# An attention, feed-forward and expert kernel: hidden features of the early expert tiles turned by transfers, routing tables made in parts

## Chip, cores and metric

The kernel runs on one core of a Trainium2 chip. The metric is device time in microseconds, the median of the runs of a kernel. All arithmetic is in float32.

## What is computed

The reference, cut to what matters:

```python
# x: 2048 x 256, ctx: 1601 x 256
y = layernorm(x)                                 
y = layernorm(y + causal_attention(y, y, y), g1, beta1)
y = layernorm(y + attention(y, ctx, ctx), g2, beta2)
y = layernorm(y + relu(y @ w1 + b1) @ w2 + b2, g3, beta3)
x = x + y
h = layernorm(x)
probs = softmax(h @ wg.T)                         # 8 experts
topk_w, topk_idx = top_k(probs, 2)
topk_w = topk_w / sum(topk_w)
out = x + sum over the 2 chosen e of topk_w[e] * ((silu(h @ w1[e].T) * (h @ w3[e].T)) @ w2[e].T)   # w1, w3: 512 x 256 each
```

The change is in the last line, the experts, and in the tables that say which rows go to which expert.

## The kernel before

**Blocks.** The 2048 rows are four blocks of 512. Self-attention, cross-attention and the feed-forward part run block by block. The last block's feed-forward runs in two halves of 256 rows (`ffn`, line 592); its second half is the last thing on TensorE before the expert stage, and its normalisations on VectorE and GpSimd run on into that stage.

**Routing.** `route(b)` (line 699) makes a block's logits on TensorE and its two best experts on VectorE. For the last block it first turns the normalised rows with eight TensorE transposes (line 256) that ScalarE copies out of PSUM (line 257), then makes 16 small matmuls (line 711). `place(b)` (line 768) counts with two matmuls (lines 772 and 773) at which slot of its expert each row goes, and returns eight scatters ("puts", line 805) on GpSimd's queue that write the rows into the table `slots` in DRAM. From the counts, `tables_0`, `tables_a` and `tables_b` (lines 919, 927 and 933) make small tables on VectorE: for every tile of 128 slots its expert and its first row. `tables_b` is for the tiles that can be filled only when the last block is placed.

**The expert stage.** `run` (line 1192) goes over 37 tiles: a0 to a16 (numbers 0 to 16; full tiles that are known before the last block), p0 to p7 (17 to 24; partly filled ones) and b0 to b11 (25 to 36). For tile n it does, in the order of the program: the first hidden product h1 (`hidden`, four matmuls of 128 x 512, line 1084) and its SiLU on ScalarE into g; the fetch of tile n+3 on SyncE's queue (`fetch`, four transfers of rows and one of weights and row numbers); the second hidden product h3; on VectorE the multiplication of g by h3; then `between(n)`, the turn of tile n+2's rows (`turn_in`, a VectorE transpose within blocks of 32 x 32, line 1066), and the loading of expert numbers for tile n+1.

**Turning g.** The output product (`product`, line 1122, eight matmuls into y) needs g with its 512 features on the partitions. The kernel before has two ways:

- `turn_out` (line 1114): four TensorE transposes into a PSUM bank gtp, and a copy by ScalarE. TensorE does them between h1(n) and h3(n) for tile n-1, and product n-1 follows h3(n).
- `send_across` and `turn_sent` (lines 1096 and 1106): four transfers of 64 KB from ScalarE's queue carry quarters of g across the partitions into gb, and VectorE turns gb in blocks of 32 x 32 into gT. Here g is written with its features in another order, so SiLU and multiplication work on rearranged views. The product of tile n-2 comes between h1(n) and h3(n): one tile later than in the first way.

The set `sent` (line 1023) says which tiles go the second way: 8 to 35. Tile 36, the last, always goes the first way.

**Who orders what.** TensorE's order is the program's throughout. On VectorE, ScalarE and SyncE the compiler chooses the order by its own estimate, until `run` reaches tile SENT = 8 (line 1198); from there on these three run in the program's order. GpSimd's order is the compiler's throughout, with `tc.issue_after` setting single instructions behind others.

**The last block among the tiles.** `between(n)` (line 1249) calls `route` of the last block at n = LATE = 2 and `place` and `tables_b` at n = PUT = 4, so that TensorE meets the routing work after those tiles. Of the eight puts, two are issued after each of tiles 5 to 8, behind the latest indirect add of a product into the output (line 1135, GpSimd's queue). Tables of the last block are first used by the fetch of tile 17, in the turn of tile 14.

**SyncE.** `keep` (line 681) writes the sums xf of the last block to the output; the adds of all expert tiles wait for it.

Of the kernel before, what the change touches and what calls it, by code (L numbers as in the profile page):

```python
# [15 lines left out]
P = 128  # L16
# [3 lines left out]
def xattn_ffn_moe(  # L20
# [46 lines left out]
    NBT = NF_MAX - NA  # L67
    AHEAD = 3
    MORE = 2
    LATE = 2  # L70

# [764 lines left out]
    def filled(n, b):  # L838


        cnt = table(f"cnt{n}", [E])
        nc.vector.tensor_sub(cnt, carry[b], region)
        ge = table(f"ge{n}", [E, NT], tag="ge")
        nc.vector.tensor_tensor(
            ge,
            cnt.unsqueeze(2).to_broadcast([P, E, NT]),
            full.unsqueeze(1).to_broadcast([P, E, NT]),
            ALU.is_ge,
        )
        f = table(f"f{n}", [E])  # L850
        nc.vector.reduce_sum(f, ge, axis=AX.X)
        return f
# [21 lines left out]
    def first_rows(n, ex, k, many):  # L874
        r = table(f"row{n}", [many])
        nc.vector.scalar_tensor_tensor(r, ex, float(REG), k, ALU.mult, ALU.add)
        return r
# [11 lines left out]
    def behind_done(n, f, done, many):  # L889


        left = table(f"left{n}", [E])
        nc.vector.tensor_sub(left, f, done)
        run = running(n, left)
        ex, k = spread(n, run, left, many)
        same = table(f"same{n}", [many, E])
        nc.vector.tensor_tensor(
            same,
            ex.unsqueeze(2).to_broadcast([P, many, E]),
            expert.unsqueeze(1).to_broadcast([P, many, E]),  # L900
            ALU.is_equal,
        )
        skip = summed(
            f"skip{n}", same, done.unsqueeze(1).to_broadcast([P, many, E]), [many, E]
        )
        nc.vector.tensor_add(k, k, skip)
        return ex, first_rows(n, ex, k, many), taken(n, left, run, many, done)

    def taken(n, left, run, many, done=None):

        d = table(f"done{n}", [E])
        nc.vector.tensor_sub(d, left, run)
        nc.vector.tensor_scalar_add(d, d, float(many))
        nc.vector.tensor_scalar_max(d, d, 0.0)
        nc.vector.tensor_tensor(d, d, left, ALU.min)
        if done is not None:
            nc.vector.tensor_add(d, d, done)
        return d
# [8 lines left out]
    def tables_a(done):  # L927
        f = filled("a", NB - 2)
        many = NA - NA0
        ex, r, done = behind_done("a", f, done, many)  # L930
        return at_weights("exa", ex, many), whole("rowa", r, many, P), done

    def tables_b(done):
        f = filled("b", NB - 1)

        part = first_rows("p", expert, f, E)
        few = table("few", [E])
        nc.vector.tensor_scalar(few, f, 0.5, None, ALU.is_le)
        swap = table("swap", [E])
        nc.vector.tensor_scalar(swap, part, -1.0, float(DUMMY // P), ALU.mult, ALU.add)  # L940
        nc.vector.tensor_mul(swap, swap, few)
        rarely = table("rarely", [E])
        nc.vector.tensor_scalar(rarely, part, float(DUMMY // P), None, ALU.add)
        nc.vector.tensor_add(part, part, swap)
        nc.vector.tensor_sub(rarely, rarely, part)
        some = table("some", [E])
        nc.vector.tensor_sub(some, carry[NB - 1], region)
        nc.vector.tensor_mul(some, some, few)
        rare = table("rare", [2])
        nc.vector.reduce_sum(rare[:, 0:1], some, axis=AX.X)  # L950
        ex, r, _ = behind_done("b", f, done, NBT)

        none = table("none", [NBT])
        nc.vector.tensor_scalar(none, ex, float(E), None, ALU.is_ge)
        nc.vector.tensor_sub(ex, ex, none)


        n = NBT - 1
        there = table("there", [2])
        nc.vector.tensor_scalar(there[:, 0:1], none[:, n:], -1.0, 1.0, ALU.mult, ALU.add)  # L960
        nc.vector.tensor_sub(there[:, 1:2], r[:, n:], part[:, E - 1 :])
        nc.vector.tensor_mul(there[:, 1:2], there[:, 1:2], there[:, 0:1])
        nc.vector.tensor_add(part[:, E - 1 :], part[:, E - 1 :], there[:, 1:2])
        m = NBT - 1 - MORE
        nc.vector.tensor_scalar(rare[:, 1:], none[:, m : m + 1], -1.0, 1.0, ALU.mult, ALU.add)
        any_rare = table("any_rare", [1])
        nc.vector.reduce_max(any_rare, rare, axis=AX.X)
        nc.vector.tensor_scalar_min(any_rare, any_rare, 1.0)
        miss = table("miss", [NBT])
        nc.vector.tensor_scalar(miss, r, -1.0, float(DUMMY // P), ALU.mult, ALU.add)  # L970
        nc.vector.tensor_mul(miss, miss, none)
        nc.vector.tensor_add(r, r, miss)
        return (
            at_weights("exb", ex, NBT),
            whole("rowb", r, NBT, P),
            at_weights("exp", ex[:, n:], 1),
            whole("rowp", part, E, P),
            whole("rowr", rarely, E, P),
            whole("rare", any_rare, 1, 1),
        )  # L980


    tabs, routed = {}, {}
# [33 lines left out]

    sure = NA + E + NBT - 1 - MORE


    PUT, SENT = LATE + 2, LATE + 6
    late_puts, added = [], []
    sent = range(SENT, sure - 1)

    def fetch(n, name, at):
        r = nc.sync.value_load(at, min_val=0, max_val=DUMMY)
# [165 lines left out]
    def run(first, end, between):  # L1192


        behind = {}
        for n in range(first, end + 1):
            name, _, _, _, into = tiles[min(n, end - 1)]
            if n == SENT:

                by_hand = {nc.vector.engine, nc.scalar.engine, nc.sync.engine}  # L1200
                ctx.enter_context(tc.manual_schedule(engines=by_hand))
            if n < end:
                w = ws.pop(n)
                h1, h3 = bank_s(f"h1_{name}"), bank_s(f"h3_{name}")
                hidden(name, xT[n], w, 0, h1)
                g = mp.tile([P, I], F32, tag="g", name=f"g_{name}")
                if n in sent:
                    silu = nc.scalar.activation(
                        g.rearrange("p (q c r) -> p c q r", q=NQ, r=Q),
                        h1.rearrange("p (c q r) -> p c q r", q=NQ, r=Q),  # L1210
                        AF.Silu,
                    )
                else:
                    silu = nc.scalar.activation(g, h1, AF.Silu)
                acted.append(silu.ins)
                if n + AHEAD < end:
                    fetch_tile(n + AHEAD)
            if n == end and n - 2 in behind:
                product(*behind.pop(n - 2))
            if n - 1 in sent:  # L1220
                gb = crossed_g
            elif n > first:
                gT = turn_out(last[0], last[2])
            if n - 2 in behind:
                product(*behind.pop(n - 2))
            if n < end:
                hidden(name, xT.pop(n), w, 1, h3)
                if n in sent:
                    nc.vector.tensor_mul(
                        g.rearrange("p (q c r) -> p q c r", q=NQ, r=Q),  # L1230
                        g.rearrange("p (q c r) -> p q c r", q=NQ, r=Q),
                        by_quarter(h3),
                    )
                    crossed_g = send_across(name, g)
                else:
                    nc.vector.tensor_mul(g, g, h3)
            if n - 1 in sent:
                behind[n - 1] = (*last[:2], turn_sent(last[0], gb), *last[3:])
            elif n > first:
                product(last[0], last[1], gT, *last[3:])  # L1240
            if n < end:
                between(n)
                if n + 2 < end:
                    turn_tile(n + 2)
                if n + 1 < end:
                    expert_of(n + 1)
                last = (name, at_token.pop(n), g, w, into)

    def between(n):
        if n == LATE:  # L1250
            route_at(NB - 1)


        for put in late_puts[:2]:
            with tc.issue_after(added[-1]):
                put()
        del late_puts[:2]
        if n == PUT:
            late_puts.extend(place_at(NB - 1))
            names = ("exb", "rowb", "exp", "rowp", "rowr", "rare")  # L1260
            tabs.update(zip(names, tables_b(tabs["done"])))
        if n == NA + E:
            tabs["rare"] = nc.values_load(tabs["rare"][0:1, :], min_val=0, max_val=1)  # L1263

# [62 lines left out]
```

## Time and profile before

| what | us |
|---|---|
| median of 3 runs | 658.37 (658.06 to 660.43) |
| the profiled execution | 660.39 |
| its span, first to last instruction | 658.7 |
| start of the expert stage's first product | 437.72 |
| start of tile 9's first hidden product | 490.69 |
| start of the last product on TensorE | 641.52 |

The mean granted TensorE clock over the span is 0.991 of full speed. In the timelines the columns are start, length, engine, line, operation, names as out<-in, count, and in brackets the idle time of the engine just ahead and what ended it. PE is TensorE, PEld its weight loads, DVE VectorE, ACT ScalarE, POOL GpSimd; SPq and ACTq are the DMA issues of SyncE and ScalarE. Lengths of successive matmuls overlap, so that the time TensorE spends on a group is the distance of two starts. Numbers n in names are left out: h_a is a hidden product of any a tile.

### The profile page before, as it was taken

How to read it: one execution, taken by the hardware profiler on the slowest of the kernel's cores; microseconds unless marked ns; L12 is line 12 of the kernel's file. 1: busy time of each engine (PE TensorE's matmuls, PEld its weight loads, DVE VectorE, ACT ScalarE, POOL GpSimd, SP SyncE). 2: the span in 40 equal slices, each digit the busy share in tenths (PEclk: the TensorE clock that was granted, in tenths of full speed). 3: DMA queues.
4: the chain of work that ended last, by engine and by line, in shares of the span. 5: the costliest groups of instructions: out<-in, count | busy, mean ns of one | idle time of the engine just before them, and what ended most of it. 6: DMA issues, size and time to landing. Idle time of an engine off the chain costs nothing. (4 is left out here: it accounts for less than half of the span.)

```text
span 658.7 us, 8201 instructions
## 1 busy us (share of the span) xinstructions
PE 628.7 (95%) x2252; PEld 407.5 (62%) x2252; DVE 324.1 (49%) x995; ACT 143.5 (22%) x254; POOL 170.2 (26%) x240
## 2 busy tenths in 40 slices
PE   5999999999999999999999999999999999999980
PEld 3666654667855687467854688876565555555550
DVE  5845074134173566816686377737623434433430
ACT  2111123251023500325023420333211111111110
POOL 4312010002050021710245022443263322222231
PEclk9999999999999999999999999999999999999996
DMA  8999929001950002200212004953355555555431
GB/s 209 270 256 321 292 71 291 0 1 32 272 175 1 0 15 81 67 31 0 66 54 75 0 9 138 344 129 65 56 110 116 97 97 99 99 106 101 88 56 18
DMA packets 100559, 70.96 MB, mean 108 GB/s; under 512 B 38365, under 2 KB 94878, under 8 KB 100510
## 3 DMA queue, kind: packets, MB, share of 16 engines
q1 hardware_dynamic: 77518, 53.96, 30.5%
q0 software_dynamic: 6864, 9.08, 8.3%
q10 hardware_dynamic: 16128, 7.35, 4.0%
q8 instruction: 21, 0.34, 0.2%
q14 instruction: 28, 0.23, 0.1%
HBM read 27.98 MB, written 29.27 MB: 87 GB/s over the span
## 5 line engine op out<-in xcount | busy, mean ns | idle before, releaser
L233 POOL TENSOR_TENSOR rs<-ve,neghalf 128x1 f32<-128x1 f32 x80 | 47.9, 605 | 221.5 <-DVE ve L231 212.8
L497 PE MATMUL co<-z_sb,raw 128*128 128x257 f32 (+1 forms) x416 | 91.4, 380 | 0.0
L452 PE MATMUL cs<-yT,zT_sb 128*128 128x512 f32 (+1 forms) x208 | 90.4, 593 | 0.0
L497 PEld LDWEIGHTS co<-z_sb,raw 128*128 128x128 f32 (+1 forms) x416 | 78.7, 190 | 11.3
L452 PEld LDWEIGHTS cs<-yT,zT_sb 128*128 128x128 f32 (+1 forms) x208 | 38.5, 186 | 47.7 <-issue 46.1
L389 PE MATMUL acc<-y,pT 128*128 128x257 f32 x272 | 65.8, 382 | 2.1 <-POOL pT L376 2.1
L389 PEld LDWEIGHTS acc<-y,pT 128*128 128x128 f32 x272 | 51.1, 190 | 21.6 <-issue 11.5
L1084 PE MATMUL h_a<-wi,xT_a 128*128 x136 | 62.5, 594 | 0.0
L630 PE MATMUL fo<-w_sb,fhs 128*128 128x256 f32 x256 | 61.1, 380 | 0.0
L608 PE MATMUL fh<-yT,w_sb 128*128 128x512 f32 (+1 forms) x160 | 60.9, 508 | 0.0
L630 PEld LDWEIGHTS fo<-w_sb,fhs 128*128 128x128 f32 x256 | 48.2, 190 | 16.1 <-issue 9.3
L459 ACT COPY raw<-cs 128x512 f32<-128x512 f32 (+1 forms) x52 | 30.4, 585 | 92.0 <-PE cs L452 92.0
L486 DVE TENSOR_TENSOR raw<-raw,top_row 128x512 f32<-128x512 f32 (+1 forms) x52 | 31.7, 685 | 27.2 <-ACT top_row L483 27.2
L364 PE MATMUL ss<-y0T,y0T 128*128 128x512 f32 x96 | 44.6, 592 | 0.0
L1084 PE MATMUL h_b<-wi,xT_b 128*128 x96 | 43.3, 592 | 0.0
L374 ACT ACTIVATE pT<-ss 128x512 f32<-128x512 f32 (+3 forms) x40 | 21.3, 532 | 94.3 <-PE ss L364 94.3
L617 ACT ACTIVATE fhs<-fh,b_sb 128x512 f32<-128x512 f32 (+1 forms) x40 | 23.9, 598 | 77.4 <-PE fh L608 77.4
L1135 POOL DMA_INDIRECT out_dram<-yw_a,at_a x17 | 26.6, 1565 | 53.5 <-DVE yw_a L1133 23.6
L462 DVE TENSOR_TENSOR top<-cs,top 128x512 f32<-128x512 f32 (+1 forms) x44 | 30.2, 687 | 20.5 <-ACT raw L459 19.9
L608 PEld LDWEIGHTS fh<-yT,w_sb 128*128 128x128 f32 x160 | 29.6, 190 | 16.9 <-issue 13.1
L1084 PEld LDWEIGHTS h_a<-wi,xT_a 128*128 128x128 f32 x136 | 25.1, 190 | 21.8 <-issue 21.0
L1125 PE MATMUL y_a<-wo,gT_a 128*128 x136 | 32.5, 382 | 1.2 <-DVE gT_a L1108 1.1
(255 smaller groups left out, 732.2 us busy)
## 6 DMA issues: line engine op xcount, KB each, us to landing
slots<-empty SPq DMA_DIRECT2D x8, 2064.0 KB
wo<-in_m2T_dram SPq DMA_DIRECT2D x8, 512.0 KB
wi<-in_m1T_dram SPq DMA_DIRECT2D x4, 1024.0 KB
wi<-in_m3T_dram SPq DMA_DIRECT2D x4, 1024.0 KB
gb_b<-g_b ACTq DMA_DIRECT2D x44, 64.0 KB
gb_a<-g_a ACTq DMA_DIRECT2D x36, 64.0 KB
xs_a<-slots SPq DMA_DIRECT2D x68, 32.0 KB
tb_y<-ya SPq DMA_DIRECT2D x16, 128.0 KB
```

Source lines behind the costliest of these rows:

```text
L233: raised.append(nc.gpsimd.tensor_tensor(rs, ve, neghalf, ALU.pow).ins)
L364: nc.tensor.matmul(s[:, :n], lhsT=y0T[kt // TPB][:, c, (kt % TPB) * P : (kt % TPB + 1) * P], rhs=y0T[b][:, c, j0 * P :], start=(c == 0), s ...
L389: nc.tensor.matmul(acc[j][:, : D + 1], lhsT=pt[:, (j - j0) * P : (j - j0 + 1) * P], rhs=y0[kt], start=(kt == 0), stop=(kt == b * TPB + j),)
L452: nc.tensor.matmul(s[:n, :], lhsT=zT_sb[:, c, k * P : k * P + n], rhs=yT[b][:, c, :], start=(c == 0), stop=(c == ND - 1),)
L459: acted.append(nc.scalar.copy(raw[:n, k, :], s[:n, :]).ins)
L462: topped = nc.vector.tensor_tensor(top[:n, :], s[:n, :], raw[:n, 0, :] if k == 1 else top[:n, :], ALU.max).ins
L486: nc.vector.tensor_sub(e, e, top_row[: keys(k), :])
L497: nc.tensor.matmul(acc[j][:, : D + 1], lhsT=raw[:n, k, j * P : (j + 1) * P], rhs=z_sb[:n, k, :], start=(k == 0), stop=(k == NK - 1),)
L608: nc.tensor.matmul(s[:, :n], lhsT=w1_sb[:, c, f * P : (f + 1) * P], rhs=yT[b][:, c, q0 : q0 + n], start=(c == 0), stop=(c == ND - 1),)
L630: nc.tensor.matmul(acc[j], lhsT=h[:, i * P : (i + 1) * P], rhs=w2_sb[:, f, :], start=(f == 0 and i % 2 == 0), stop=(f == NF - 1), skip_gro ...
L1084: nc.tensor.matmul(into, lhsT=xT[:, c, :], rhs=wi[n, c].rearrange("p e i -> p (e i)")[:, bass.ds(w[0], I)], start=(c == 0), stop=(c == ND ...
L1125: nc.tensor.matmul(y[:, :D], lhsT=gT[:, i, :], rhs=wo[:, bass.ds(w[1] + i * D, D)], start=(i == 0), stop=(i == NI - 1),)
```

## The change

All expert tiles but the last turn g by transfers and VectorE (`sent` is now 0 to 35). The routing of the last block comes one tile later (LATE = 3, so route after tile 3, place after tile 5, two puts after each of tiles 6 to 9). `tables_b` is now a generator in four parts, which `between` runs after tiles 6, 7, 8 and 9; the "done" table of the last block, which nothing reads, is no longer made. VectorE, ScalarE and SyncE run in the program's order from tile PUT = 5 on. In that order the turn of tile n+2's rows now comes ahead of `between(n)`.

```diff
-    LATE = 2
+    LATE = 3
...
-        return ex, first_rows(n, ex, k, many), taken(n, left, run, many, done)
+        return ex, first_rows(n, ex, k, many), left, run
...
     def tables_a(done):
         f = filled("a", NB - 2)
         many = NA - NA0
-        ex, r, done = behind_done("a", f, done, many)
+        ex, r, left, run = behind_done("a", f, done, many)
+        done = taken("a", left, run, many, done)
         return at_weights("exa", ex, many), whole("rowa", r, many, P), done
...
         nc.vector.reduce_sum(rare[:, 0:1], some, axis=AX.X)
-        ex, r, _ = behind_done("b", f, done, NBT)
+        yield
+        ex, r, _, _ = behind_done("b", f, done, NBT)
+        yield
...
         nc.vector.tensor_add(r, r, miss)
-        return (
-            at_weights("exb", ex, NBT),
-            whole("rowb", r, NBT, P),
-            at_weights("exp", ex[:, n:], 1),
-            whole("rowp", part, E, P),
-            whole("rowr", rarely, E, P),
-            whole("rare", any_rare, 1, 1),
-        )
+        yield
+        tabs["exb"], tabs["rowb"] = at_weights("exb", ex, NBT), whole("rowb", r, NBT, P)
+        tabs["exp"], tabs["rowp"] = at_weights("exp", ex[:, n:], 1), whole("rowp", part, E, P)
+        tabs["rowr"] = whole("rowr", rarely, E, P)
+        tabs["rare"] = whole("rare", any_rare, 1, 1)
...
-    PUT, SENT = LATE + 2, LATE + 6
-    late_puts, added = [], []
-    sent = range(SENT, sure - 1)
+    PUT = LATE + 2
+    late_puts, added, last_tables = [], [], []
+
+    sent = range(sure - 1)
...
-            if n == SENT:
+            if n == PUT:
...
             if n < end:
-                between(n)
                 if n + 2 < end:
                     turn_tile(n + 2)
+                between(n)
...
         if n == PUT:
             late_puts.extend(place_at(NB - 1))
-            names = ("exb", "rowb", "exp", "rowp", "rowr", "rare")
-            tabs.update(zip(names, tables_b(tabs["done"])))
+            last_tables.append(tables_b(tabs["done"]))
+        elif last_tables:
+            next(last_tables[0], None)
```

## The prediction

> **What bounds the kernel now.** I read the engine totals first, then the busy time by stage, then the timelines of TensorE, VectorE and the queues around the change, and last the list of who waited for whom.
>
> ```profile
> PE 628.7 (95%) x2252; PEld 407.5 (62%) x2252; DVE 324.1 (49%) x995; ACT 143.5 (22%) x254; POOL 170.2 (26%) x240
> ```
>
> TensorE is busy for 95% of the span, so a change pays only where it takes work off TensorE or a wait out of its row. The stages, as busy time of each engine (last columns: granted clock, share of the DMA engines, GB/s):
>
> ```profile
> 437.70:452.30 14.60, 14.60 (x49) 8.33 (x48) 9.33 (x29) 3.05 (x6) 3.80 (x7) 1.00 0.13 25
> 452.30:455.90 3.60, 3.17 (x25) 2.57 (x24) 1.85 (x4) 2.58 (x5) 1.77 (x4) 1.00 0.65 158
> 455.90:490.70 34.80, 34.35 (x127) 21.05 (x127) 18.12 (x107) 9.02 (x15) 15.88 (x13) 1.00 0.46 75
> 490.70:638.40 147.70, 144.45 (x441) 81.20 (x439) 59.39 (x111) 16.72 (x28) 45.38 (x30) 1.00 0.53 98
> ```
>
> The change touches the expert stage's first 53 us (437.7 to 490.7, tiles 0 to 7). There TensorE stands idle for less than 1 us at the full granted clock (1.00): 34.80 less 34.35 is 0.45 us, and 3.60 less 3.17 is 0.43 us. What can be won is therefore nearly all removed work. The TensorE timeline shows that work, and the stage that already runs in the new manner:
>
> ```profile
> 437.72 5.31 PE L1084 MATMUL h_a<-wi,xT_a 128*128 x12
> 442.87 0.60 PE L1117 MATMUL gtp_a<-ident,g_a 128*128 128x128 f32 x4
> 443.31 1.88 PE L1084 MATMUL h_a<-wi,xT_a 128*128 x4
> ...
> 475.56 0.65 PE L1117 MATMUL gtp_a<-ident,g_a 128*128 128x128 f32 x4 [0.45 <-DVE rare_i L883]
> ...
> 490.69 5.31 PE L1084 MATMUL h_a<-wi,xT_a 128*128 x12
> 496.28 1.99 PE L1125 MATMUL y_a<-wo,gT_a 128*128 x8 [0.28 <-DVE gT_a L1108]
> ```
>
> Starts tell the price, since the ends overlap: four transposes take 443.31 - 442.87 = 0.44 us, one hidden product (four matmuls) takes (442.87 - 437.72) / 3 = 1.717 us. The eight matmuls of y take the same 1.72 (445.03 to 446.75 in the same timeline).
>
> **What is removed.** Tiles 0 to 7 lose their 32 transposes: 8 x 0.44 = -3.5 us of TensorE. TensorE's order is written by hand, so nothing moves into the gap. Eight ScalarE copies of 0.58 us go too; ScalarE has 9.02 of 34.80 us busy there, so they are worth nothing. The 0.45 us wait at 475.56 belongs to the table burst on VectorE (467.8 to 475.5, which held back the multiply of tile 6); split in parts, it goes: -0.45 (bounds -0.45 and 0). The five VectorE instructions that made the last "done" table (some 0.16 us each) go as well, and count nothing since VectorE is not the bound. The 0.28 at 496.28 is the first wait of the transfer route; I keep it.
>
> **What is added: eight trips.** Each tile gets four transfers from ScalarE's queue, and a VectorE turn. How long a trip takes is read from the first one of before:
>
> ```profile
> 489.24 0.69 DVE L1229 TENSOR_TENSOR g_a<-g_a,h_a 128x512 f32<-128x512 f32 x1 [3.46 <-PE h_a L1084]
> 489.95 2.60 ACTq L1100 DMA_DIRECT2D gb_a<-g_a  x4
> 495.51 0.71 DVE L1108 STREAM_TRANSPOSE gT_a<-gb_a 128x512 f32<-128x512 f32 x1 [0.44 <-DMA gb_a<-g_a]
> ```
>
> Multiply ends 489.93, issue ends 492.55, landing 495.51 (2.96 after the issue), product at 496.28, 0.77 after the turn began. From the multiply's end to the product that is 6.35 us. In the steady row four pieces of TensorE work lie between a tile's second hidden product and its y (6.9 us), which just covers multiply and trip. At tile 0 there is no earlier y to fill in: h1(1), h3(1) and h1(2) are all. TensorE is free at 437.72 + 5 x 1.717 = 446.3. The multiply of tile 0 ended at 442.11 (441.42 + 0.69, waiting for TensorE alone). For the landing there are two rows: 2.96 us above, with eight scatters of the router under way, and 1.86 us in a quiet stretch:
>
> ```profile
> 431.02 0.82 SPq L1032 DMA_DIRECT2D xs_a<-slots  x2
> ...
> 433.70 0.45 DVE L1066 STREAM_TRANSPOSE xT_a<-xs_a 128x256 f32<-128x256 f32 x1 [1.11 <-DMA xs_a<-slots]
> ```
>
> From 437.7 to 452.3 the DMA share is 0.13, so I stand near the quiet row: 442.11 + 2.60 + 1.86 + 0.77 = 447.3 against 446.3, a bubble of 1.0; with the other row 2.1. Taken: +1.2 us. It is paid once, since afterwards the products run two tiles behind.
>
> [...]
>
> **Tiles 0 to 4, which the compiler still orders.** Before, it laid no trips there; now VectorE gets four turns (0.71 each) and four waits on transfers among the normalisations of the last half block (9.33 of 14.60 us busy), and ScalarE gets 4 x 2.6 us of issuing among the copies of the router. Behind a turn that waits on VectorE stand the next multiply and the normalisations; behind those, the router's transposes on TensorE, the last write of xf on SyncE, and the expert tiles' adds into the output on GpSimd. Cover: the router moves from after tile 2 to after tile 3, so that TensorE reaches it at about 437.72 + 10 x 1.717 + 1.2 = 456.1 instead of 452.3, 3.8 us later, while its last rows were ready at 453.3; three turns (2.1) and a wait of 1.0 just fit. The copies of the router on ScalarE may stand behind tile 3's issues: nothing, or 2.6 us. Bounds 0 and +3; no gain is possible, as the idle there was 0.43 and stays or grows. Nearest is the lower end, since the order before shows only 0.2 us waits for these copies: +0.9.
>
> **Tiles 5 to 9 by written order.** The place step and the tables' parts hold about 14, 13, 13, 12 and 16 VectorE instructions. The burst took 7.1 us without tile 6's multiply for 70 of them, 0.10 each, interleaved; in a dependent chain such as the router's (457.45 to 459.01) they follow each other at 0.22. So a part costs 1.2 to 3.5 us. The room is what VectorE idles in a steady tile, 1.76 + 1.29 = 3.05 us:
>
> ```profile
> 503.48 0.48 DVE L1133 TENSOR_SCALAR yw_a<-y_a,at_a 128x256 f32<-128x256 f32 x1 [1.76 <-PE y_a L1125]
> 505.25 0.69 DVE L1229 TENSOR_TENSOR g_a<-g_a,h_a 128x512 f32<-128x512 f32 x1 [1.29 <-PE h_a L1084]
> ```
>
> Only the dependent price of the largest part exceeds it, by 0.5, and the turn that releases the next product ends some 0.3 before it is needed. Bounds 0 and +1; taken +0.1. Turning tile n+2 ahead of the part keeps that tile off this account. The eight scatters now run beside trips in tiles 6 to 9; before, tile 8's trip beside them cost 0.28. Three more such: 0 to +0.9, taken +0.3. GpSimd itself does no more; its scatters end one tile (5.2 us) after 495.8 at the latest, and the first rows that need them were fetched at 506.9. SyncE issues the same loads, by hand three tiles earlier; its lead of two tiles hides that.
>
> **The sum.** -3.5 - 0.45 + 1.2 + 0.9 + 0.1 + 0.3 = -1.4 us. The profiled execution took 660.39 us (span 658.7 and 1.7 around it), so it would take 659.0; it stands 2.0 above the median shown. At the median: 658.37 - 1.4 = 657.0. The bounds add to -3.95 + 1.0 = -2.95 and to -3.5 + 2.1 + 3 + 1 + 0.9 = +3.5, so 655.4 to 661.9.
>
> **Rivals.** (1) *The bubble is hidden.* TensorE has no spare work to put there, which speaks against it; but a landing of less than 1 us after the last issue, pieces landing while later ones are issued, and compiler-ordered tiles that run like the steady row would leave only the gains: -3.95, 654.4. Chance 0.13. (2) *The compiler's order makes VectorE and ScalarE the bound of tiles 0 to 4.* It sets VectorE's turn of tile 0 ahead of the multiply of tile 1; that multiply, ready at 445.4, waits until 447.3, its trip lands late, and y(1) stalls again (about 1.9); the normalisations queue behind, and the router's copies behind 2.6 us of issues. 658.37 - 3.95 + 2.1 + 1.9 + 2.6 = 661.0. It decides the sign once its loss, over the bubble, passes some 2 us. For it: the old order already left VectorE idle for 4.08 us ahead of tile 0's multiply with normalisations pending. Against it: that cost TensorE nothing. Chance 0.27. (3) *The written order of the parts delays multiplies:* every multiply of tiles 6 to 9 late by 0.6 through dependent chains and hiccups like the 0.37 us one in the burst: 657.0 + 2.4 = 659.4. Chance 0.10. The forecast keeps 0.50.
>
> **Chances.** This kernel's runs spread by 0.36%, so 0.5% (3.3 us: 655.1 and 661.7) is what can be told from no change. Faster: most of rival 1 and a sliver of the forecast, 0.14. Slower: the bad half of rival 2, 0.14. Within: 0.72. Cases of both signs hold most of the chance: the forecast's own range is 655.4 to 659; for eight in ten, 654.6 to 662.0.
>
> **What would show it.** Right: no gtp groups but that of the last tile; one idle of 1 to 2 us on TensorE, ahead of the first y, put down to gT; tiles 5 to 9 at 5.17 us; the router's transposes starting near 456. Wrong: idle on TensorE before the router's transposes or its logits, put down to ScalarE's yT copies or to late ya rows (rival 2), idle before the y of tiles 5 to 9 put down to gT (rival 3), or no idle before the first y (rival 1). Any change before 437 us would also upset the sum.

## The result, and the profile after

| | us |
|---|---|
| before, median of 4 runs | 658.21 (657.94 to 660.43) |
| after, median of 4 runs | 665.56 (664.51 to 666.07) |
| ratio, 95% interval | 1.010 (1.0079 to 1.012) |
| profiled execution of after, its span | 665.35, 663.6 |

The change makes the kernel 7.35 us slower. The forecast said 657.0 and the range ended at 662.0: it was wrong, and by more than any of its rivals allowed.

The page of after, from the engine totals and the row of the granted clock over 40 slices:

```profile
PE 629.5 (95%) x2220; PEld 406.4 (61%) x2220; DVE 332.3 (50%) x998; ACT 139.7 (21%) x246; POOL 170.3 (26%) x240
...
PEclk9999999999999999999999999998899999999996
```

32 TensorE instructions are gone (2252 to 2220), and yet TensorE is busy for 0.8 us longer, not 3.5 us shorter. Its share of the span still reads 95%. The two eights in the clock row (the 28th and 29th slice, some 448 to 481 us) say why: a matmul at a lower clock took longer here (four of a hidden product 3.55 us at 0.50, against 1.717 at 1.00), and the profile counts it as busy while it does. The TensorE timeline of the first five tiles:

```profile
436.77 8.75 PE L1085 MATMUL h_a<-wi,xT_a 128*128 x20
448.37 2.57 PE L1126 MATMUL y_a<-wo,gT_a 128*128 x8 [2.85 <-DVE ve L231]
450.73 4.76 PE L1085 MATMUL h_a<-wi,xT_a 128*128 x8
455.33 1.89 PE L1126 MATMUL y_a<-wo,gT_a 128*128 x8
457.06 1.88 PE L1085 MATMUL h_a<-wi,xT_a 128*128 x4
458.77 0.60 PE L256 MATMUL pt_xn<-ident,ya 128*128 128x128 f32 x4
459.62 0.71 PE L256 MATMUL pt_xn<-ident,ya 128*128 128x128 f32 x4 [0.24 <-ACT yT L257]
462.85 3.19 PE L711 MATMUL lp<-wg_sb,yT 128*128 128x8 f32 x16 [2.52 <-ACT yT L257]
465.89 3.76 PE L1085 MATMUL h_a<-wi,xT_a 128*128 x4
469.44 2.23 PE L1126 MATMUL y_a<-wo,gT_a 128*128 x8
```

There are two gaps: 2.85 us ahead of the first y and 2.52 us ahead of the router's logits. Look also at the lengths. A hidden product (four matmuls) should take 1.717 us from start to start. The two at 450.73 take 4.60 us together instead of 3.43, and the one at 465.89 takes 3.55. The stretches between these starts, as windows (columns: stretch and length, busy us and instructions of PE, PEld, DVE, ACT and POOL, granted clock, DMA share, GB/s):

```profile
445.35:448.37 3.02, 0.17 (x1) 0.00 (x1) 2.58 (x10) 0.00 (x0) 0.51 (x1) 1.00 0.29 51
448.37:450.73 2.36, 2.36 (x8) 1.97 (x9) 1.68 (x6) 0.60 (x1) 1.20 (x2) 0.77 0.42 118
450.73:455.33 4.60, 4.60 (x10) 1.96 (x8) 3.51 (x10) 0.00 (x0) 1.50 (x4) 0.75 0.50 138
458.77:462.85 4.08, 1.32 (x10) 0.77 (x8) 1.64 (x3) 1.07 (x4) 1.56 (x1) 1.00 0.56 93
462.85:465.89 3.04, 3.04 (x16) 3.04 (x17) 0.00 (x0) 1.50 (x2) 0.00 (x0) 0.57 0.42 96
465.89:469.44 3.55, 3.55 (x5) 1.49 (x6) 2.99 (x14) 1.51 (x2) 0.00 (x0) 0.50 0.21 39
469.44:471.51 2.07, 2.07 (x9) 1.80 (x8) 0.55 (x5) 0.60 (x1) 0.00 (x0) 0.83 0.04 2
```

The clock is full (1.00) in both gaps and falls behind them (0.77 and 0.75; 0.57, 0.50 and 0.83). What it costs is estimated as (1 - clock) x length, since 4.60 x 0.75 = 3.45 us is the 3.43 of two hidden products: 2.36 x 0.23 + 4.60 x 0.25 = 1.7 us behind the first gap, and 3.04 x 0.43 + 3.55 x 0.50 + 2.07 x 0.17 = 3.4 us behind the second.

With that the account closes. From the start of the first hidden product to the end of tile 9's second one, before takes 494.12 - 437.72 = 56.40 us and after 499.68 - 436.77 = 62.91, which is 6.51 more:

| term | predicted us | measured us |
|---|---|---|
| 32 transposes and the wait behind the table burst | -3.95 | -3.95 |
| bubble ahead of the first y | +1.2 | +3.0 |
| waits at the router (before: 0.42 in all) | +0.9 | +2.3 |
| tiles 5 to 9 | +0.4 | 0.0 |
| half clock behind the two gaps | no term | +5.1 |
| sum | -1.4 | +6.5 |

The last product on TensorE starts 210.23 us after the first hidden one, before 203.80: 6.4 more. The profiled executions as a whole are 5.0 us apart (665.35 and 660.39), since after reached its expert stage 0.95 us earlier; the rest of the medians' 7.35 comes from where they lie among their runs, before 2.2 us above its median and after 0.2 below.

**Why the first gap is 3.0 us.** The VectorE timeline:

```profile
440.48 0.69 DVE L1230 TENSOR_TENSOR g_a<-g_a,h_a 128x512 f32<-128x512 f32 x1 [3.04 <-PE h_a L1085]
...
446.30 0.68 DVE L1230 TENSOR_TENSOR g_a<-g_a,h_a 128x512 f32<-128x512 f32 x1
446.89 0.42 DVE L227 BATCH_NORM_STATS2 st<-xf 128x6 f32<-128x256 f32 x1
447.23 0.41 DVE L227 BATCH_NORM_STATS2 st<-yb 128x6 f32<-128x256 f32 x1
447.56 0.17 DVE L229 BATCH_NORM_AGGREGATE mv<-st 128x2 f32<-128x6 f32 x1
447.64 0.68 DVE L1109 STREAM_TRANSPOSE gT_a<-gb_a 128x512 f32<-128x512 f32 x1
```

The turn of tile 0 ends at 448.32, and the product starts at 448.37. (The profile puts the wait down to a normalisation, ve; the turn is what ended just ahead of it.) No idle time stands ahead of the turn. Its data were there: the transfer queue of ScalarE (q10) moved its last packet for tile 0 at 445.4 and none from then until 448.3. The turn stood behind tile 1's multiply and three instructions of the last block's normalisation. That order is the compiler's.

**Why the second gap is 2.5 us.** ScalarE, whose queue issues the transfers between its own copies:

```profile
441.20 3.10 ACTq L1101 DMA_DIRECT2D gb_a<-g_a  x4
...
459.19 0.65 ACT L257 COPY yT<-pt_xn 128x256 f32<-128x256 f32 x2 [1.22 <-PE pt_xn L256]
459.76 2.62 ACTq L1101 DMA_DIRECT2D gb_a<-g_a  x4
462.42 0.65 ACT L257 COPY yT<-pt_xn 128x256 f32<-128x256 f32 x2 [2.59 <-issue]
```

Two of the router's four copies run, then tile 3's four issues hold ScalarE for 2.62 us, then come the other two copies. The logits start at 462.85, just after the third copy ends (462.42 and 0.37 us long), and the last of them need the fourth.

### The profile page after: what moved, and what is told of

Its sections match the earlier page's. It is cut to its first block, busy times and chain, and to the rows that moved or that the text cites. A ratio compares the mean times of both kernels' runs of the same rounds, so it can differ in the third digit from the quotient of the medians.

```text
span 663.6 us, 8186 instructions
## 1 busy us (share of the span) xinstructions
PE 629.5 (95%) x2220; PEld 406.4 (61%) x2220; DVE 332.3 (50%) x998; ACT 139.7 (21%) x246; POOL 170.3 (26%) x240
## 5 line engine op out<-in xcount | busy, mean ns | idle before, releaser
L1085 PE MATMUL h_a<-wi,xT_a 128*128 x136 | 64.4, 617 | 0.0
L1085 PEld LDWEIGHTS h_a<-wi,xT_a 128*128 128x128 f32 x136 | 26.8, 199 | 26.1 <-issue 25.2
```

Source lines behind the costliest of these rows:

```text
L1085: nc.tensor.matmul(into, lhsT=xT[:, c, :], rhs=wi[n, c].rearrange("p e i -> p (e i)")[:, bass.ds(w[0], I)], start=(c == 0), stop=(c == ND ...
```

## The experiments

Every ratio is to the kernel before, run on the same chip beside it; brackets hold the 95% interval. Diffs are against the kernel after unless it is said otherwise. In them a "trip" is the way by transfers and VectorE.

### One gap at a time

**Tile 0 by TensorE again**, so that the first gap has no cause:

```diff
-    sent = range(sure - 1)
+    sent = range(1, sure - 1)
```

> Tile 0 alone goes back to TensorE transposes; all else as in the changed kernel (665.6 us; the kernel before 658.2). Idle-and-clock theory: the 3.0 us gap ahead of the first y and the some 1.7 us that the half clock cost behind it both go, 0.44 us of transposes come back: about 661.3 us, granted clock 1.00 from 445 us to the router. Rival 'the gap counts, the lower clock is incidental': 3.0 less 0.44, about 663.0. Rival 'the written order and the tables' parts cost the time': no change, 665.6.

Measured: 666.81 us, 1.0117 (1.0093 to 1.014). A miss. The gap was not removed, it moved one tile on:

```profile
454.13 2.71 PE L1126 MATMUL y_a<-wo,gT_a 128*128 x8 [1.86 <-DVE gT_a L1109]
456.64 2.89 PE L1085 MATMUL h_a<-wi,xT_a 128*128 x4
```

Now tile 1 is the first whose product has no earlier one to fill in, and its turn stands behind normalisations in the same way (453.37). The hidden product behind it is stretched again (2.73 us to the next start, 459.37, at a mean clock of 0.50 from 456 to 458 us). In both executions the tile that starts the pipeline pays for it. At the router the second gap stayed, as it was meant to.

**Tile 3's transfers issued behind the router's copies**, so that the second gap has no cause:

```diff
+    def copy_row(dst, src):
+        row_copies.append(nc.scalar.copy(dst, src).ins)
...
-                transpose_to(turned(t), row(t), f"xn_{t}", nc.scalar.copy)
+                transpose_to(turned(t), row(t), f"xn_{t}", copy_row)
+            sent_late.extend(h() for h in held)
...
-    def send_across(name, g):
+    def send_across(name, g, behind=None):
...
+            with tc.issue_after(behind) if behind is not None else ExitStack():
...
-                    crossed_g = send_across(name, g)
+                    if n == LATE:
+                        held.append(lambda name=name, g=g: send_across(name, g, row_copies[-1]))
+                    else:
+                        crossed_g = send_across(name, g)
...
+                if n == LATE:
+                    crossed_g = sent_late.pop()
```

> The transfers of tile 3 are issued behind the router's four ScalarE copies. Idle-and-clock theory: the 2.5 us gap ahead of the router's logits goes, and with it the some 3.4 us of half clock behind it: about 659.7 us; the gap ahead of the first y and its slow clock stay. Rival 'the gap counts, the clock is incidental': 663.1. Rival 'written order': 665.6. If the delayed trip of tile 3 matters instead, a new wait shows ahead of y of tile 3.

Measured: 660.36 us, 1.0014 (0.9999 to 1.0028), some 5 us below the kernel after. The second gap alone, a wait of 2.5 us, was worth twice its length. TensorE's timeline in the profiled execution:

```profile
449.26 2.00 PE L1133 MATMUL y_a<-wo,gT_a 128*128 x8 [2.85 <-DVE ve L231]
...
460.10 2.10 PE L717 MATMUL lp<-wg_sb,yT 128*128 128x8 f32 x16 [0.18 <-ACT yT L702]
462.05 3.50 PE L1091 MATMUL h_a<-wi,xT_a 128*128 x4
465.39 1.89 PE L1133 MATMUL y_a<-wo,gT_a 128*128 x8
```

The logits wait 0.18 us as they did before the change. The first gap is still there, but in this execution no slow stretch follows it (a clock of 1.00 from 445 to 455 us). One follows the router: the product at 462.05 takes 3.34 us to the next start, at a clock of 0.50. The runs spread from 657.5 to 661.2 us, about as widely as those of the kernel before (656.8 to 660.4).

**Both edits together.**

> Both edits together. Idle-and-clock theory: 665.6 - 4.3 - 5.9 = about 655.4 us, below the kernel before, with no gap over 1 us on TensorE before the last tiles and the clock at 1.00 from 445 to 495 us. Rival 'gaps alone': about 660.5. Rival 'written order': 665.6.

Measured: 660.47 us, 1.0025 (1.0014 to 1.0036). A miss by 5 us: the gap ahead of tile 1's product (1.87 us, at 453.74) comes back with its own slow stretch, a mean clock of 0.64 from 453.70 to 458.50.

### The gaps filled with useless work

If it is the clock, work that nobody needs must bring time back. **24 useless transposes ahead of the first y, 20 ahead of the logits:**

```diff
+    def filler(name, groups):
+        t = bank_o(name)
+        for _ in range(groups):
+            for c in range(4):
+                nc.tensor.transpose(t[:, c * P : (c + 1) * P], ident, ident)
...
+            filler("fill1", 5)
...
+            if n == 2:
+                filler("fill0", 6)
```

> The changed kernel with useless TensorE transposes of the identity put where it sat idle: 24 (2.6 us) ahead of the first y, 20 (2.2 us) ahead of the router's logits; their results are read by nobody. Nothing waits less for it. Idle-and-clock theory: the gaps are as long as before but busy, the clock stays at 1.00 behind them, and some 1.7 + 3.4 us are won: about 660.5 us. Rival 'the clock is incidental, or set by something else': 665.6 or a little more.

Measured: 665.37 us, 1.0105 (1.0081 to 1.0128): the total was missed, and the two places have to be read apart. Windows:

```profile
444.88:447.90 3.02, 2.79 (x25) 2.54 (x24) 2.58 (x10) 0.00 (x0) 0.51 (x1) 1.00 0.29 58
447.90:449.73 1.83, 1.83 (x8) 1.63 (x9) 1.27 (x5) 0.17 (x1) 1.11 (x2) 1.00 0.34 97
449.73:453.30 3.57, 3.57 (x9) 1.36 (x8) 2.65 (x8) 0.42 (x1) 0.90 (x4) 1.00 0.60 183
...
465.34:470.57 5.23, 5.23 (x13) 3.11 (x13) 3.54 (x18) 2.11 (x3) 0.00 (x0) 0.67 0.17 30
```

At the first gap the clock stayed up. The useful work is held up for the same 3.02 us (the first y starts 11.60 us after the first hidden product, as in the kernel after), but the clock behind it stays at 1.00, and from that y to the router's transposes it is 8.92 us instead of 10.40, 1.5 us less. The execution with the issues moved had a full clock behind this gap without any filler, so one execution does not show that the filler did it. At the router the filler did not cover the wait. Tile 3's issues still stood between the copies, TensorE still idled 0.66 and 2.43 us, and from the router's first transposes to the logits it took 6.59 us instead of 4.08. The clock fell again, to 0.67, at a cost of 5.23 x 0.33 = 1.7 us instead of 3.4. What was won at the two places was lost in that longer stretch.

**The issues moved and the first gap filled**, that is the second experiment and `filler("fill0", 6)`:

> The kernel of the second experiment (tile 3's transfers behind the router's copies) with 24 useless TensorE transposes in the gap ahead of the first y. In that experiment the gap of 3 us stayed and the half clock came 3.4 us long behind the router, 1.6 us lost. Theory, the clock follows TensorE's idle time of the last several us: with the gap busy the clock stays at 1.00 through the router, 1.6 us won: ratio to before 0.999, about 658 us beside 658.5. Rival, the router's small products alone draw the clock down: the half clock stays and the time is that of the second experiment, ratio 1.0014.

Measured: 657.21 us, 0.9992 (0.9976 to 1.0009). Between this kernel and the one with the issues moved stand only 24 transposes whose result nothing reads (2.6 us of TensorE work); with them the ratio falls by 0.22%, some 1.4 us, but the two intervals overlap, so that the medians alone do not show a gain. In its profiled execution the clock is full over the whole stretch:

```profile
442.00:482.00 40.00, 38.91 (x152) 24.21 (x151) 26.16 (x95) 9.11 (x15) 14.53 (x16) 1.00 0.52 109
```

This does not show the filler at work, since the profiled execution with the issues moved had a full clock behind the unfilled gap too, and behind the router the two may differ by chance alone: the runs with the issues moved spread from 657.5 to 661.2 us. What useless work does to the clock rests on the first gap of the kernel with both fillers, in one execution.

### Which part of the change costs

**Trips from tile 4 on** (`sent = range(4, sure - 1)`, all else as after):

> The changed kernel with trips from tile 4 on; tiles 0 to 3, which lie among the normalisations and ahead of the router's copies, go back to TensorE transposes. Theory (trips in the compiler-ordered tiles make TensorE wait, waits of 2 us and more halve its clock; the written order and the parts are sound): no gap over 1 us up to the last tiles, clock 1.00 throughout, 4 x 0.44 + 0.45 = 2.2 us won against the kernel before: ratio 0.997, about 656.3 us beside 658.5. Rival 'written order and parts cost': slower than before by some us with gaps in tiles 5 to 9.

Measured: 657.45 us, 0.9986 (0.9971 to 1.0001), with a clock of 1.00 from 446 to 482 us in the profiled execution. The bound of 2 us in the expectation was the author's estimate, and the runs do not show it: 2.85 and 2.52 us in the kernel after and 1.86 us with tile 0 by TensorE were followed by 0.50, 2.85 us with the issues moved was not. **Trips only from tile 8 on, as before the change, the parts and the written order kept** (`sent = range(8, sure - 1)`):

> The other half of the change alone: tables in four parts, routing one tile later, VectorE, ScalarE and SyncE in the program's order from tile 5; trips from tile 8 as in the kernel before. Theory: only the 0.45 us wait behind the table burst can go: ratio 0.999 to 1.000, about 658.0 beside 658.5. Rival 'written order and parts cost': 660 or more, with waits of TensorE in tiles 5 to 8.

Measured: 659.27 us, 1.0014 (0.9999 to 1.003). **Only the trips, nothing else of the change** (against the kernel before):

```diff
-    sent = range(SENT, sure - 1)
+    sent = range(sure - 1)
```

> The kernel before with trips for all tiles and nothing else: router after tile 2, tables in one burst, written order from tile 8. Theory: the gap ahead of the first y (3 us) and a wait in the router's copies behind tile 2's issues (2.6 us), each with a stretch of half clock: slower than before by 5 us or more, 663 to 668. Rival 'written order costs': as the kernel before or faster, 655 to 659.

Measured: 663.38 us, 1.0089 (1.0068 to 1.011). So the loss is in the trips of tiles 0 to 3, which the compiler orders: with them 1.010, without them 0.9986. Parts and written order alone cost nothing that can be told. Without them the trips meet the table work in one piece: in the trips-only kernel a turn on VectorE is late behind the table burst, and the product of tile 4 stalls:

```profile
477.69 1.99 PE L1125 MATMUL y_a<-wo,gT_a 128*128 x8 [2.79 <-DVE gT_a L1108]
```

That gap, and the one of 2.86 us ahead of the first y (449.59), are followed by a clock of 1.00 in this execution (in every stretch from 436 to 486 us), at 661.51 the shortest of the four (up to 665.39). So a gap of this length did not lower the clock every time.

The parts-only kernel shows the reverse. It has no gap at all in these tiles, only the router's usual waits, and in the profiled execution the half clock came even so (a mean of 0.60 from 460 to 462 us and 0.55 from 462 to 464):

```profile
458.89 2.25 PE L711 MATMUL lp<-wg_sb,yT 128*128 128x8 f32 x16 [0.18 <-ACT yT L257]
461.00 3.35 PE L1085 MATMUL h_a<-wi,xT_a 128*128 x4
464.18 0.60 PE L1118 MATMUL gtp_a<-ident,g_a 128*128 128x128 f32 x4
```

From 461.00 to 464.18 is 3.18 us for a product of 1.72.

### A gap without any transfer

The transfers were still suspect: DMA traffic may lower the clock by itself. So the kernel **before** got useless ScalarE copies between the router's second and third, which delay the logits and touch nothing else:

```diff
+    def copy_row(dst, src):
+        with tc.issue_after(row_copies[-1]) if row_copies else ExitStack():
+            row_copies.append(nc.scalar.copy(dst, src).ins)
...
+                if j == 1:
+                    for _ in range(3):
+                        scr = work.tile([P, D], F32, tag="h", name="scr")
+                        copy_row(scr, w2_sb[:, 0, :])
```

> The kernel before, no trip added: three useless ScalarE copies (128x256, some 0.3 us each) stand between the router's second and third copy, so that TensorE waits about 0.8 us longer there. [...] Rival 'a wait costs its length': +0.8, ratio 1.001.

Measured with three copies: a wait of 0.75 us instead of 0.18, and 659.94 us, 1.0012 (1.0001 to 1.0023), which is about the added wait. The profiled execution, one of the long ones (661.68), has a clock of 0.50 from 457 to 460 us. The parts-only kernel had such a stretch with no added wait, so it cannot be laid to the 0.75 us. **With eight copies:**

> The same with eight copies: TensorE waits about 2.3 us longer ahead of the router's logits, without any trip. Theory: the wait of 2.3 us is followed by 3.4 to 7 us of half clock as in the changed kernel, 1.7 to 3.4 us lost: +4.0 to +5.7 us, ratio 1.006 to 1.009, granted clock 0.5 behind the logits. Rival 'a wait costs its length, the transfers lower the clock': +2.3 us, ratio 1.0035, clock 1.00.

Measured: a wait of 2.27 us, and 663.36 us, 1.0066 (1.0052 to 1.008), 4.3 us for 2.1 us of added wait. Windows:

```profile
450.90:454.73 3.83, 1.32 (x10) 0.77 (x8) 1.85 (x4) 3.41 (x12) 2.00 (x4) 1.00 0.57 147
454.73:457.49 2.76, 2.76 (x16) 2.76 (x17) 0.00 (x0) 1.50 (x2) 0.38 (x1) 0.64 0.78 98
457.49:461.90 4.41, 4.41 (x9) 2.24 (x10) 3.43 (x21) 2.11 (x3) 1.56 (x1) 0.50 0.45 74
```

The picture is that of the kernel after, with no trip in sight: full clock in the gap, then 0.64 and 0.50 behind it. In this execution the clock costs 2.76 x 0.36 + 4.41 x 0.50 = 3.2 us; with the wait that makes 5.3, 1.0 more than the medians differ by. A gap was enough here, then, with no trip near it; the trips of the kernel after only make the gaps.

### A version that beats both

If only gaps cost, the trips may stay where there is none, and the router's transposes can be taken out of the gap's way: made after tile 2, with the logits after tile 3, so that a whole hidden product hides the copies.

```diff
+    def turn_rows(b):
+        for j in range(TPB):
+            t = b * TPB + j
+            transpose_to(turned(t), row(t), f"xn_{t}", nc.scalar.copy)
...
-        if b == LAST:
-            for j in range(TPB):
-                t = b * TPB + j
-                transpose_to(turned(t), row(t), f"xn_{t}", nc.scalar.copy)
...
-    sent = range(sure - 1)
+    sent = range(4, sure - 1)
...
+        if n == LATE - 1:
+            turn_rows(NB - 1)
```

> Trips from tile 4 on, as in the fifth experiment, and the router split: its eight transposes after tile 2, its logits and the rest after tile 3, so that the copies of ScalarE are done long before and no stretch of small TensorE work is longer than 2 us. Theory: the 0.4 us of waits in the router go, and the half clock that some executions take behind the router (1.6 us) cannot come: ratio 0.996 to 0.997, below the fifth experiment's 0.9986, with a narrower spread. Rival 'the spread has another cause': ratio 0.9985, spread as before.

Measured: 657.38 us, 0.9976 (0.9965 to 0.9988): faster than before, but not told apart from the trips from tile 4 alone (0.9971 to 1.0001), so that the split by itself is not shown to pay. **The same with trips from tile 3** (`sent = range(3, sure - 1)`):

> The same with trips from tile 3 on: one more TensorE transpose group goes (0.44 us), and tile 3's issues no longer stand ahead of router copies. Theory: 0.4 us below the kernel with trips from tile 4, ratio about 0.996, no new gap. Rival 'a trip beside the router always costs': slower than that kernel by 1 us or more, with a gap ahead of the logits or of y of tile 3.

Measured: 656.19 us, 0.9957 (0.9942 to 0.9972), the fastest kernel of this study: 2.8 us below the kernel before. TensorE around the router:

```profile
453.27 0.71 PE L256 MATMUL pt_xn<-ident,ya 128*128 128x128 f32 x4 [0.24 <-ACT yT L257]
455.01 1.98 PE L1086 MATMUL h_a<-wi,xT_a 128*128 x4 [1.03 <-issue]
...
460.71 1.85 PE L712 MATMUL lp<-wg_sb,yT 128*128 128x8 f32 x16
462.42 5.40 PE L1086 MATMUL h_a<-wi,xT_a 128*128 x12
```

The logits start without a wait, and the three products behind them take 5.23 us together, 1.74 each. A gap of 1.03 us is left between the transposes and the product behind them, put down to issue; it was not tried to remove it.

## Why the prediction was wrong

**The step that failed is "Tiles 0 to 4, which the compiler still orders", and with it the bubble's size; and one term was missing.** Point by point:

- **What is removed: right.** The transposes of eight tiles are gone, and so is the wait behind the table burst. (The multiply that the burst held back was tile 5's, not tile 6's: the transposes at 475.56 turn tile 5's g. The price is the same.)
- **The bubble ahead of the first y: right mechanism, wrong size.** Taken +1.2, bounds 1.0 to 2.1, measured 3.0. The issue took 3.10 us instead of 2.60 (+0.5). The other 1.5 us, above the lower bound of 1.0, is a wait that the sum did not have: with a landing 1.86 us after the issue the turn could have begun at 444.30 + 1.86 = 446.2, and VectorE took it at 447.64. The +1.2 is the author's choice between two landings, 1.86 and 2.96 us; no run shows it, and the 3.0 stands in its place. The bounds covered two durations of the landing but no place in VectorE's queue, though the prediction itself named the normalisations there.
- **The router's copies behind tile 3's issues: seen, priced, and valued too low.** "Nothing, or 2.6 us" was the sentence; it was 2.52, ahead of the logits. The value near the lower end was read from an order that had no issues among those copies, so it said nothing about where the compiler would put them.
- **Tiles 5 to 9: right.** The hidden products start 5.18 us apart per tile (482.41, 487.59, 492.77, 497.96), so the parts delay none. The next waits for a turn are 0.26 us, ahead of the y of tile 8 (501.81), and 0.77, ahead of that of tile 10 (513.19). Rival 3's 2.4 us did not come.
- **The clock: no term.** The prediction read "granted clock 1.00" in the rows of before and carried it over to a kernel with two gaps in it. It was worth 5.1 us, the largest term of the account and most of the miss of 8.6 us: -1.4 + 1.8 + 1.4 + 5.1 - 0.4 is the +6.5 of the account (what the bubble and the router cost above the values taken, the clock, and what was taken too high at tiles 5 to 9).
- **Rival 2 had the place and not the price.** Its router term was right to 0.3 us. Its VectorE term had the order the wrong way round: the multiply of tile 1 went ahead of the turn, not behind it, and the second y (455.33) did not stall. It came to 661.0 because it too added up waits alone.
- **What would show it** served well: idle on TensorE before the logits, put down to yT, was named as the sign of rival 2.

The length of a gap alone does not tell whether the half clock comes: 2.27 us was followed by 0.50 with no trip in play, 0.75 us and the router's usual waits (0.18 and 0.24 us) were too in some executions, while the trips-only kernel passed 2.86 us and the kernel with the issues moved 2.85 us at 1.00.

## What to carry to other kernels

On this TensorE-bound kernel gaps of 2.27 and 2.52 us cost about twice their length (4.3 us for 2.1 us of added wait; some 5 us for the second gap), and one of 2.86 us was followed by a full clock: price such a gap at up to twice its length, and look at the granted clock behind it, since the busy share does not show it (95% before and after). Before a pipeline is made a stage longer, find out where it is filled: here the first trip had no earlier work to cover it, and where the compiler orders the queues, both its turn (1.5 us late) and the issues of a later one (2.62 us) landed between instructions that TensorE waited for. Where two such pieces compete, start the longer route behind the competing work (worth some 5 us here) and move the short, waiting matmuls so that a whole product lies between them and their copies (the logits then started without a wait).

## What the runs showed of the hardware

- **The clock fell behind a gap, not in it, for 3.4 or 6.8 us.** In after it was 1.00 from 445.35 to 448.37 and from 458.77 to 462.85, where the two gaps lie, and 0.50 from 449.65 to 453.06 (3.41 us) and from 463.30 to 470.13 (6.83 us). In seven other profiled executions with a slow stretch here (tile 0 by TensorE, the issues moved, both edits, both fillers, parts only, and the two with useless copies) (1 - clock) x length, added up over windows of 2 us, comes to 1.7 us for one, or 3.4; at 0.50 that is 3.4 or 6.8 us long. The shorter kind is thus estimated to cost 1.7 us.
- **Gaps of 1.86 to 2.86 us were mostly followed by 0.50.** Followed by it: 2.85 and 2.52 us in after, 1.86 and 2.06 with tile 0 by TensorE, 1.87 with both edits, 2.43 with both fillers, 2.27 with eight copies. Not followed by it: 2.85 with the issues moved, 2.86 and 2.79 in the trips-only kernel. No run was made to show what parts them.
- **It came behind the router also with little idle time.** The 3.41 us ahead of a slow stretch, and the stretch, in after (first gap) and with the issues moved (router):

```profile
446.24:449.65 3.41, 1.28 (x6) 1.15 (x7) 3.16 (x12) 0.00 (x0) 0.57 (x2) 1.00 0.34 73
449.65:453.06 3.41, 3.41 (x7) 1.83 (x6) 2.21 (x8) 0.60 (x1) 1.45 (x4) 0.50 0.50 161
...
458.34:461.75 3.41, 2.98 (x24) 2.42 (x22) 1.73 (x3) 1.68 (x5) 1.56 (x1) 1.00 0.62 125
461.75:465.17 3.42, 3.42 (x7) 1.79 (x7) 0.57 (x3) 2.55 (x3) 0.00 (x0) 0.50 0.79 139
```

  In after TensorE idles 2.13 us there, with the issues moved 0.43 us, beside 1.65 us of logits, 16 products of 8 columns. The parts-only kernel had the half clock with the router's usual waits alone, and the kernel with trips from tile 4 had none behind the same router. That the small products bring it is not shown.
- **With useless matmuls in the first gap the clock stayed at 1.00.** In the profiled execution with both fillers it was 1.00 from 447.90 to 453.30, where after had 0.77 and 0.75 in the same work, and that work was done 1.5 us sooner. It is one execution, and with the issues moved the clock was 1.00 there without them. The 1.4 us in the ratios to before is within their noise.
